# Moving the second routing exponential and two expert weight conversions on ScalarE

## Chip, cores and metric

The kernel runs on one core of a Trainium2 chip. The metric is the device time of one launch in microseconds (us). Engines are named as in the profile: PE is TensorE's matrix multiplication and PEld its weight load, DVE is VectorE, ACT is ScalarE, POOL is GpSimd, SP is SyncE, which here only issues transfers.

## What is computed

One decoder layer on 1,024 tokens (16 sequences of 64) of width 256: self-attention with 16 heads, then cross-attention, then a mixture of experts. The change lies in the last part, which in the reference is, cut to what matters:

```python
scores = softmax(xt @ Wg.T)                          # T x 16
gmask  = the 2 best of 4 groups of 4 experts
topi   = top 4 of the scores inside these groups
combine[t, topi] = scores[t, topi]
h = silu(xt @ W1[e].T) * (xt @ W3[e].T)              # 176 wide, each expert e
y = sum over e of combine[:, e] * (h @ W2[e].T)
z = silu(xt @ Ws1.T) * (xt @ Ws3.T) @ Ws2.T          # two shared experts, 352 wide
x = x + y + z
```

## The kernel before

**Precision.** Most products are made from two fp32r parts of each operand: a high part, written by ACT as a rounding copy, and a low part, written by DVE (or POOL) as source minus high part. A product is then three matmuls: high x high, high x low, low x high. `parts_of` (line 111) makes the two parts of an activation: the cast is line 112, the subtraction line 113. `weight_parts` (line 276) loads one expert's weights in one transfer of 640 KB on SP's queue (line 277), casts all 1,280 columns on ACT (line 278) and subtracts in two pieces (line 283): the first 768 columns on DVE, the last 512 on DVE for the first three experts and on POOL for all later ones.

**Order of the work.** The kernel is written as one program; a planner with a time model of its own sorts it, and each engine then runs its instructions strictly in the order so fixed. `tc.issue_after(ins)` adds an edge: what is traced in the block stays behind `ins` on the engine of `ins`, and nothing is said of other engines. The helper `after` takes several such instructions. So an edge permits or forbids places; it doesn't fix one.

**Routing.** Tokens are handled in two halves of 512. `choose` (from line 774) ranks the experts from the raw logits, so the softmax isn't needed for the choice. `send` scatters the token rows to per-expert slots in memory by indirect transfers that POOL issues (line 864), four for each of the four choices and half. `weights_of_choices` (line 891) makes the softmax: a maximum over the logits (line 897), a subtraction (line 899), the Exp on ACT (line 900), a sum, a reciprocal and a dozen small DVE operations (lines 902 to 919). Its results are used when the experts' outputs are added at the end, and by the dense expert's adds of that half.

**Around the change.** After cross-attention the two shared experts of the second half run: `shared_up` (Silu at line 937, a copy at 941), `shared_hidden` (product at 948, `parts_of`), `shared_output` (adds at line 970). The last of the 16 experts is dense (computed for all tokens): `dense_up`, `dense_gated`, `dense_out` (adds at line 974). Then 15 experts follow in a software pipeline over `e`, each on 384 slots:

- `expert_inputs` (from line 1309): a load `xr` of 408 KB on SP's queue (line 1314), which waits for the scatters of its choices; six PE transposes (line 1324); two casts (112), two subtractions (113).
- `expert_weights`, i.e. `weight_parts`; the raw weights have two buffers, so a load waits until the subtractions of two experts earlier are done.
- `expert_hidden` (from line 1333): 18 matmuls (through line 104), a Silu of the gate (line 1342), a DVE product (1343), `parts_of`, the same for the remaining 48 rows (Silu 1345, product 1346).
- `send_outputs` (from line 1352): 15 matmuls (line 104), three copies (line 1358), three indirect transfers that POOL issues (line 1363).

Before the change the weights of expert 1 and of expert 2 (the second and third; counting starts at 0) are cast after the latest second Silu (line 1345), because of `tc.issue_after(silus[-1])`; the second half's `weights_of_choices(1)` is traced as a whole in step `e == 1`, behind expert 0's gate.

Of the kernel before, what the change touches and what calls it, by code (L numbers as in the profile page):

```python
# [30 lines left out]
ALU = mybir.AluOpType  # L31
# [11 lines left out]
E, INTER, NGRP, TOPK, TOPKG = 16, 176, 4, 4, 2  # L43
# [28 lines left out]
def decoder_layer(ctx: ExitStack, tc: tile.TileContext, a: dict, out: bass.AP):  # L72
# [21 lines left out]
    @contextmanager  # L94
    def after(*instructions):

        with ExitStack() as order:
            for ins in instructions:
                order.enter_context(tc.issue_after(ins))
            yield  # L100
# [8 lines left out]
        return [(left[0], right[0]), (left[0], right[1]), (left[1], right[0])]  # L109

    def parts_of(src, hi, lo, eng=None):
        nc.scalar.copy(hi, src)
        return (eng or nc.vector).tensor_tensor(lo, src, hi, ALU.subtract).ins


    x_pairs = [acts.tile([128, 2, D], F32, tag=f"x{n}", name=f"x{n}") for n in range(NI // 2)]
# [198 lines left out]
    with ExitStack() as attn:  # L315
# [572 lines left out]
            nc.vector.tensor_tensor(w, w, p, ALU.mult)  # L888
            return w

        def weights_of_choices(half):


            shape = [128, 4, E]
            lg = logits[half]
            m = fs.tile([128, 4], F32, tag="r_m", name="r_m")
            nc.vector.tensor_reduce(m, lg, AX.X, ALU.max)
            p = fs.tile(shape, F32, tag=f"r_p{half}", name=f"r_p{half}")
            nc.vector.tensor_tensor(p, lg, m.unsqueeze(2).broadcast_to(shape), ALU.subtract)
            exps.append(nc.scalar.activation(p, p, AF.Exp).ins)  # L900
            s = fs.tile([128, 4], F32, tag="r_s", name="r_s")
            nc.vector.tensor_reduce(s, p, AX.X, ALU.add)
            nc.vector.reciprocal(s, s)
            nc.vector.tensor_tensor(p, p, s.unsqueeze(2).broadcast_to(shape), ALU.mult)
            sel = selected[half]
            last = fs.tile([128, 4], F32, tag=f"cl{half}", name=f"cl{half}")
            nc.vector.tensor_tensor(last, sel[:, :, E - 1], p[:, :, E - 1], ALU.mult)
            nth = fs.tile(shape, F32, tag="slot", name="nth_back")
            nc.vector.tensor_tensor(
                nth, places[half], sel[:, :, E - 1 :].broadcast_to(shape), ALU.add  # L910
            )
            ch = choices(nth, sel)
            kept = fs.tile(shape, F32, tag="slot", name="kept")
            nc.vector.scalar_tensor_tensor(kept, over[half], 0.5, p, ALU.is_lt, ALU.mult)
            nc.vector.tensor_tensor(
                ch, ch, kept.unsqueeze(1).broadcast_to([128, TOPK, 4, E]), ALU.mult
            )
            w = fs.tile([128, TOPK, 4], F32, tag=f"cw{half}", name=f"cw{half}")
            nc.vector.tensor_reduce(w, ch, AX.X, ALU.add)
            return w, last, p  # L920
# [23 lines left out]
        def shared_hidden(k, g, up, pool, h_p=None):  # L944

            n = min(128, SHI - k * 128)
            h = pool.tile([128, 512], F32, tag=f"rt{k % 2}0", name="sgh")[:n]
            nc.vector.tensor_tensor(h, up, g, ALU.mult)
            h_p = [
                t[:n]  # L950
                for t in h_p
                or [
                    pool.tile([128, 512], F32R, tag=f"c_t{m}", name=f"sh{m}", bufs=4)
                    for m in range(2)
                ]
            ]
            lows.append(parts_of(h, h_p[0], h_p[1]))
            return h_p

        def shared_output(half, hs):  # L960
            for k in range(4):
                ps = mm_tile(cols=D)
                cols = slice(k * 128, (k + 1) * 128)
                pairs = []
                for t, h_p in enumerate(hs):
                    n = min(128, SHI - t * 128)
                    pairs += three([p[:, cols] for p in h_p], [w[:n, t, :] for w in ws2_p])
                matmuls(ps, pairs)
                i = half * 4 + k
                nc.vector.tensor_tensor(x[i], ps, x[i], ALU.add)  # L970
# [10 lines left out]
        with (  # L981
# [150 lines left out]
            def dense_gated(g, up, g2, up2):  # L1132
                h_p = [
                    xa.tile([128, 512], F32R, tag=f"roped1{n}", name=f"dense1{n}", bufs=1)
                    for n in range(2)
                ]
                h_p.append(xa.tile([128, 512], F32R, tag="q_r", name="dense2"))
                nc.vector.tensor_tensor(g, up, g, ALU.mult)
                parts_of(g, h_p[0], h_p[1])
                nc.vector.tensor_tensor(g2[:64], up2[64:], g2[64:], ALU.mult)  # L1140
                parts_of(g2[:64], h_p[2][:64], h_p[2][64:])
                return h_p
# [18 lines left out]
            for n in range(len(units) + 2):  # L1161
# [85 lines left out]
                if n == 8:  # L1247
                    w_last = dense_weights()
                    with after(exps[-1]):
                        routed.append(weights_of_choices(0))  # L1250
                if n == 9:
                    rows[1] = [
                        xw.tile([128, 3, 2, 2, DC], F32, tag="w_s", name="rows1")
                        .rearrange("p a b c d -> p (a b c d)")[:, : 2 * ROW]
                        .rearrange("p (a b) -> p a b", a=2)
                        for _ in range(2)
                    ]
                    normed[1] = layernorm_t(3, (1,), token_rows(1))[0]
                    high = highs[-1]
                    scored, placed, aimed = choose(1)  # L1260
                    sh = [
                        xb.tile([128, 2, 2, 4 * HQ], F32R, tag=f"w_q{m}", name=f"sh{m}")
                        .rearrange("p a b c -> p (a b c)")
                        for m in range(2)
                    ]
                    hs = []
                    for k in range(3):
                        with after(*pn_turned[(0 if k else 1) :]):
                            up = shared_up(0, k, xa)
                            part = [t[:, k * 512 : (k + 1) * 512] for t in sh]  # L1270
                            hs.append(shared_hidden(k, *up, xa, part))
                    with tc.issue_after(rstds[-1]):
                        send(0, (2,), [lows[-1]])
                    with after(projected, scaled[-1]):
                        shared_output(0, hs)
                    send(0, (3,), [high])
                    send(1)
                    with after(high):
                        dense_ups = dense_up(0, turned[-1], scored, scored)
                    with after(aimed, scored):  # L1280
                        ups = [shared_up(1, 0, xa)]
                    with after(aimed, placed):
                        ups.append(shared_up(1, 1, xa))
                        hs = [shared_hidden(k, *ups[k], xa) for k in range(2)]
                        ups.append(shared_up(1, 2, xa))
                        hs.append(shared_hidden(2, *ups[2], xa))
                        h_p = dense_gated(*dense_ups)
                        shared_output(1, hs)
                        dense_out(h_p, 0, range(4), add_last)

# [121 lines left out]
    for e in range(E + 1):  # L1412
        if e in (1, 2):

            low = lows[-1]
            hs[e - 1] = expert_hidden(ws[e - 1], xs[e - 1][0], SLOTS)
        if e < E - 1:
            low = lows[-1]
            with tc.issue_after(up_done[0] if e in (1, 2) else low):
                xs[e] = expert_inputs(e)  # L1420
            if e >= 1:
                with tc.issue_after(low), tc.issue_after(silus[-1]):
                    ws[e] = expert_weights(a["W123"][e], nc.vector if e < 3 else nc.gpsimd)
        if e == 1:
            with tc.issue_after(gated[0]), tc.issue_after(silus[-1]):
                routed.append(weights_of_choices(1))
        if 0 <= e - 1 < E - 1 and e > 2:
            hs[e - 1] = expert_hidden(ws[e - 1], xs[e - 1][0], SLOTS)
        if e - 2 >= 0:
            if e == E:  # L1430

                with tc.issue_after(gated[0]):
                    h_p = dense_hidden(w_last, 1, 0)
            last = send_outputs(e - 2, ws.pop(e - 2), hs.pop(e - 2), xs.pop(e - 2)[1])
            if e - 2 == E - TOPK - 2:
                short = slots_are_short()
            k = e - 2 - (E - 1 - TOPK)
            if k >= 0:
                got[k] = load_outputs(k)
# [140 lines left out]
```

## Time and profile before

| | us |
|---|---|
| median of 3 runs (555.78 to 557.23) | 556.84 |
| the profiled execution's own time | 558.26 |
| its span, first to last instruction | 556.1 |
| busy of that span: PE / DVE / ACT / POOL | 524.9 / 382.5 / 304.3 / 228.7 |
| second half's shared experts, from their first matmul | 419.7 on |
| expert 0's first up matmul | 439.59 |
| experts 3 to 14 in a steady rhythm, about | 460 to 540 |

A line of a timeline gives the start in us from the span's start, the duration, engine, line, operation, what it writes <- what it reads (names without buffer numbers), the shape, how many were merged, and in brackets how long the engine was idle before and what ended that wait. "issue" there is a wait that the profile can't name. Times are of one profiled execution.

### The profile page before, as it was taken

To read this page: it belongs to the slowest core of one execution; us is meant where nothing else is said; L and a number is where in the kernel's file an instruction comes from. 1 tells how busy PE (TensorE), PEld (TensorE's weight loads), DVE (VectorE), ACT (ScalarE), POOL (GpSimd) and SP (SyncE) were. 2 spreads that over 40 slices of the span, in tenths; PEclk is the share of its full clock that TensorE was granted. 3 is DMA by queue.
4 is the path that set the end of the run, shared out by engine and by line. 5 is a ranking of instruction groups with operands and counts; after the bars stand their busy time and mean duration, and the time that the engine had idled before them with its cause. 6 is when DMAs were issued, how large, how long until landed. Compare 5 with 4: busy or idle time off the path is not lost.

```text
span 556.1 us, 10815 instructions
## 1 busy us (share of the span) xinstructions
PE 524.9 (94%) x4013; PEld 442.1 (80%) x4013; DVE 382.5 (69%) x863; ACT 304.3 (55%) x764; POOL 228.7 (41%) x213
## 2 busy tenths in 40 slices
PE   7999999999999989999999999999999879999982
PEld 6888898998989876668677686685886769999971
DVE  5465573754736799657475566758768688999967
ACT  3667575585665520625545364455735377777651
POOL 4260500101000016444342533543534737888873
PEclk9999999999999999999999999999999989999995
DMA  8553432834200779472010000000511577777366
GB/s 227 158 170 109 140 95 77 209 97 133 77 1 1 230 203 306 124 230 73 1 62 12 8 1 1 0 30 2 174 52 71 195 235 265 238 235 262 123 250 217
DMA packets 44263, 70.84 MB, mean 127 GB/s; under 512 B 11824, under 2 KB 25232, under 8 KB 44208
## 3 DMA queue, kind: packets, MB, share of 16 engines
q1 hardware_dynamic: 39376, 58.71, 35.3%
q0 software_dynamic: 3696, 10.36, 4.8%
q10 hardware_dynamic: 1136, 1.05, 0.6%
q8 instruction: 33, 0.54, 0.4%
q14 instruction: 22, 0.18, 0.1%
HBM read 48.61 MB, written 21.86 MB: 127 GB/s over the span
## 4 chain that ended last, share of the span: by engine, by line


## 5 line engine op out<-in xcount | busy, mean ns | idle before, releaser
L1014 POOL TENSOR_TENSOR roped<-rt,rt 128x512 f32<-128x512 f32 x48 | 61.8, 1309 | 52.6 <-DVE rt L1006 51.6
L104 PE MATMUL mm<-xn,w_q 128*128 128x512 f32 x288 | 72.6, 402 | 0.5 <-ACT xn L222 0.5
L1006 DVE TENSOR_TENSOR rt<-mm,rope_q 128x512 f32<-128x512 f32 x96 | 61.0, 680 | 10.8 <-PE mm L104 10.4
L104 PEld LDWEIGHTS mm<-xn,w_q 128*128 128x128 f32 x288 | 52.6, 188 | 14.3 <-issue 1.2
L104 PE MATMUL mm<-xs,w 128*128 128x384 f32 x270 | 53.8, 347 | 6.9 <-issue 2.3
L1363 POOL DMA_INDIRECT yd<-y,to x45 | 47.8, 1062 | 20.7 <-ACT y L1358 7.1
L325 DVE TENSOR_REDUCE sm_m<-at 128x8 f32<-128x512 f32 x32 | 21.9, 684 | 47.9 <-PE at L582 47.1
L104 PEld LDWEIGHTS mm<-xs,w 128*128 128x128 f32 x270 | 46.7, 192 | 9.0 <-issue 5.1
L331 ACT ACTIVATE p<-at,sm_m 128x64 f32<-128x64 f32 x128 | 38.2, 343 | 14.9 <-DVE sm_m L329 12.8
L523 POOL TENSOR_TENSOR wv<-code,scale 128x512 fp32r<-128x512 f32 x7 | 9.1, 1294 | 89.2 <-DMA scale<-in_scales 59.6
L1032 PE MATMUL mm<-roped,w_s 128*64 128x512 f32 x192 | 44.3, 599 | 0.2 <-DVE rt L1006 0.2
L360 ACT COPY pt<-at 64x512 f32<-64x512 f32 x32 | 18.6, 582 | 40.0 <-PE at L352 40.0
L565 ACT ACTIVATE qT<-mm,bqkv 128x512 f32<-128x512 f32 x32 | 21.8, 688 | 33.7 <-PE mm L104 33.7
L104 PE MATMUL mm<-wv,xn 128*128 128x256 f32 x256 | 36.2, 288 | 0.0
L104 PE MATMUL mm<-wo,o 128*128 128x256 f32 x256 | 34.1, 286 | 2.1 <-DVE x L624 2.1
L104 PE MATMUL av<-w,hp 128*128 128x256 f32 x225 | 35.1, 290 | 0.3 <-ACT y L1358 0.3
L104 PEld LDWEIGHTS mm<-wo,o 128*128 128x128 f32 x256 | 31.7, 191 | 3.7 <-DVE x L624 3.2
L104 PE MATMUL mm<-xn,wk 128*128 128x512 f32 x128 | 34.2, 399 | 0.0
L104 PE MATMUL mm<-xn,wq 128*128 128x512 f32 x128 | 33.2, 398 | 0.2
L343 POOL TENSOR_TENSOR pn<-p,sm_s 128x512 f32<-128x512 f32 x14 | 14.6, 1044 | 45.3 <-DVE sm_s L339 45.3
L104 PEld LDWEIGHTS mm<-wv,xn 128*128 128x128 f32 x256 | 32.5, 189 | 0.7
L601 PE MATMUL av<-pt,v 128*128 128x128 f32 x256 | 31.2, 275 | 1.0 <-DVE o L611 1.0
(219 smaller groups left out, 1184.3 us busy)
## 6 DMA issues: line engine op xcount, KB each, us to landing
w<-in_W SPq DMA_DIRECT2D x15, 640.0 KB
code<-in_codes SPq DMA_DIRECT2D x32, 256.0 KB
scale<-in_scales SPq DMA_DIRECT2D x32, 256.0 KB
xr<-xd SPq DMA_DIRECT2D x15, 408.0 KB
xd<-zeros SPq DMA_DIRECT2D x8, 720.0 KB
yd<-zeros SPq DMA_DIRECT2D x8, 512.0 KB
got<-yd SPq DMA_DIRECT2D x16, 256.0 KB
wq<-in_Wq SPq DMA_DIRECT2D x4, 512.0 KB
```

What stands on the lines that cost most here:

```text
L104: m = nc.tensor.matmul(ps, lhsT=l, rhs=r, start=(n == 0), stop=(n == len(pairs) - 1))
L325: nc.vector.tensor_reduce(m, sc, AX.X, ALU.max)
L331: last = nc.scalar.activation(p[:, b], sc[:, b], AF.Exp, bias=m[:, b : b + 1], accum_out=s[:, b : b + 1])
L343: .tensor_tensor(pn, p, s.unsqueeze(2).broadcast_to(shape), ALU.mult)
L360: nc.scalar.copy(pt[:S, :, 0, :], ps[:S])
L523: mults[n] = eng.tensor_tensor(w, *loaded[gr].pop(n), ALU.mult).ins
L565: nc.scalar.activation(qk[which][:, half * 512 : (half + 1) * 512], ps, AF.Identity, bias=bqkv[:, which, h : h + 1],).ins
L601: nc.tensor.matmul(av[:, k * 128 : (k + 1) * 128], lhsT=v[:, i, k0 : k0 + HD], rhs=pt[:, i].rearrange("p a q -> p (a q)"), start=True, sto ...
L1006: factors = nc.vector.tensor_tensor(mt, ps3, rope_table(t, 2 * ab + k), ALU.mult)
L1014: nc.gpsimd.tensor_tensor(r.rearrange("p (b s) -> p b s", s=S), one, two, op)
L1032: nc.tensor.matmul(ps[h // 2][(h % 2) * 64 : (h % 2) * 64 + 64], lhsT=w_s[:, t, blk, ab, :], rhs=roped[2 * t + ab], start=first[h], stop=l ...
L1363: sent = nc.gpsimd.indirect_dma_start(out=yd[: (E - 1) * SLOTS + min(TOPK, E - 1 - e) * NT], out_offset=bass.IndirectOffsetOnAxis(ap=to[:, ...
```

## The change

`weights_of_choices` is cut in two: `exps_of_choices` (maximum, subtraction, Exp) and the rest. For the first half both are called where the whole was. For the second half `exps_of_choices(1)` is called between the dense expert's gate and the shared experts' output, behind four instructions: the cast of the last shared hidden part, the dense gate's last cast and last subtraction, and the latest Silu. The casts of expert 1's and expert 2's weights get other edges: for expert 1 the cast must follow the last cast of expert 0's inputs instead of expert 0's second Silu; for expert 2 it must follow the last cast of expert 0's hidden part instead of expert 1's second Silu. Later experts keep their edges.

```diff
     def parts_of(src, hi, lo, eng=None):
-        nc.scalar.copy(hi, src)
-        return (eng or nc.vector).tensor_tensor(lo, src, hi, ALU.subtract).ins
+        high_last[0] = nc.scalar.copy(hi, src).ins
+        low_last[0] = (eng or nc.vector).tensor_tensor(lo, src, hi, ALU.subtract).ins
+        return low_last[0]
+
+    high_last, low_last = [None], [None]
...
-        def weights_of_choices(half):
-
+        def exps_of_choices(half):
 
             shape = [128, 4, E]
             lg = logits[half]
...
             exps.append(nc.scalar.activation(p, p, AF.Exp).ins)
+            return p
+
+        def weights_of_choices(half, p):
+
+
+            shape = [128, 4, E]
             s = fs.tile([128, 4], F32, tag="r_s", name="r_s")
...
-                        routed.append(weights_of_choices(0))
+                        routed.append(weights_of_choices(0, exps_of_choices(0)))
...
                         hs.append(shared_hidden(2, *ups[2], xa))
+                        order = [high_last[0]]
                         h_p = dense_gated(*dense_ups)
+
+                        with after(*order, high_last[0], low_last[0], silus[-1]):
+                            p_last = exps_of_choices(1)
                         shared_output(1, hs)
...
         if e in (1, 2):
 
-            low = lows[-1]
+            low, cast = lows[-1], high_last[0]
             hs[e - 1] = expert_hidden(ws[e - 1], xs[e - 1][0], SLOTS)
+            if e == 2:
+                cast = hidden_high
+            hidden_high = high_last[0]
         if e < E - 1:
...
             if e >= 1:
-                with tc.issue_after(low), tc.issue_after(silus[-1]):
+
+                with tc.issue_after(low), tc.issue_after(cast if e < 3 else silus[-1]):
                     ws[e] = expert_weights(a["W123"][e], nc.vector if e < 3 else nc.gpsimd)
         if e == 1:
             with tc.issue_after(gated[0]), tc.issue_after(silus[-1]):
-                routed.append(weights_of_choices(1))
+                routed.append(weights_of_choices(1, p_last))
```

## The prediction

> **What bounds the kernel now.** First the busy time in stretches of 10 us, to see where any engine has room. The columns are the stretch, its length, then busy us and instruction count of PE, PEld, DVE, ACT and POOL, the granted clock of PE, the DMA share and GB/s.
>
> ```profile
> 440.00:450.00 10.00, 8.08 (x48) 7.05 (x47) 6.86 (x21) 6.19 (x11) 6.81 (x7) 1.00 0.78 261
> 450.00:460.00 10.00, 7.60 (x41) 6.77 (x41) 7.51 (x18) 7.03 (x13) 2.96 (x3) 0.83 0.77 248
> 460.00:470.00 10.00, 10.00 (x71) 9.97 (x70) 8.40 (x16) 7.46 (x18) 7.63 (x7) 1.00 0.69 241
> 479.00:540.00 61.00, 59.23 (x407) 57.34 (x407) 54.16 (x94) 42.49 (x94) 50.79 (x43) 1.00 0.65 222
> ```
>
> From 460 on PE is nearly always busy, and in the 61 us from 479 POOL has 43 instructions with 10.2 us between them, 0.24 each, which is the gap (0.16 to 0.30) that it leaves between any two: POOL is full there as well. So the rhythm of the later experts has no slack, and what counts is when it starts. Between 440 and 460 PE idles 1.92 + 2.40 = 4.3 us, and for a part of that time its clock is low. That is the place of the change. Next, ACT's timeline there, of which the lines that carry the argument are:
>
> ```profile
> 447.41 0.51 ACT L112 CAST hp<-h 64x384 fp32r<-64x384 f32 x1
> 447.94 1.28 ACT L900 ACT_TABLE_LOAD   x1
> 449.31 0.26 ACT L900 ACTIVATE r_p<-r_p 128x64 f32<-128x64 f32 x1
> 449.59 1.28 ACT L1342 ACT_TABLE_LOAD   x1
> 450.88 0.49 ACT L1342 ACTIVATE g<-mm 128x384 f32<-128x384 f32 x1
> 451.40 0.48 ACT L1345 ACTIVATE g<-mm 64x384 f32<-64x384 f32 x1
> 451.90 1.26 ACT L278 CAST w<-w 128x1280 fp32r<-128x1280 f32 x1
> 453.07 0.47 ACT L112 CAST xs<-at 128x384 fp32r<-128x384 f32 x1
> ...
> 457.68 1.26 ACT L278 CAST w<-w 128x1280 fp32r<-128x1280 f32 x1 [2.40 <-DMA w<-in_W]
> ```
>
> ACT is never idle from 447.41 to 453.5, and expert 2's input cast (453.07) is last in that row. PE's timeline shows who waits for it, and SP's when expert 3's weights are asked for:
>
> ```profile
> 450.17 0.82 PE L1324 MATMUL at<-ident,xr 128*128 128x128 f32 x6
> 450.74 0.72 PE L104 MATMUL av<-w,hp 128*128 128x256 f32 x4
> 453.59 0.80 PE L104 MATMUL mm<-xs,w 128*128 128x384 f32 x3 [2.13 <-ACT xs L112]
> ...
> 446.64 4.39 SPq L1314 DMA_DIRECT2D xr<-xd  x2
> 451.54 0.33 SPq L277 DMA_DIRECT2D w<-in_W  x1
> ```
>
> Expert 2's tokens are transposed by 451.0 but cast only at 453.07. Expert 3's weights, asked for at 451.54, let ACT cast them only at 457.68.
>
> **The change, part by part.** *The Exp's removal from 447.94.* Two table loads and the Exp, 1.28 + 0.26 + 1.28 with their small gaps, hold ACT from 447.94 to 450.88, 2.94 us. Not all is a gain: expert 1's gate product, which the Silu at 450.88 needs, ends at about 449.65 by PE's timeline (the ninth of the matmuls from 447.18 and two of those from 449.12), so the Silu alone gains 1.2 us. The rest of the hole serves the next edit.
>
> *Expert 2's weight cast ahead of expert 1's Silus.* It may now follow the cast at 447.41. Its data were asked for at 440.22, and the DMA share shows that load done before 445. So it fits from 447.94 to 449.20, into the hole, costs nothing there, and leaves 451.90. Then Silus at 449.66 and 450.36, input cast at 450.84 instead of 453.07: 2.23 us. If the planner left the cast where it is, only the Exp's 1.2 us would remain. Its low part (two DVE instructions of 0.94 and 0.68, overlapping to 1.55 us) moves along; DVE has 2.5 us idle between 450 and 460 and 3.1 in the ten before.
>
> *Expert 1's weight cast ahead of expert 0's Silus.* Its data were loaded at 396.75. ACT is idle from 440.28 to 442.55 and takes the 1.26 us there. After the Silu at 443.19 the input casts are then free of it, and DVE's 1.55 us for its low part (444.98 to 446.54, right in front of the inputs' low part that PE waits for until 447.18) moves to 441.5 to 443.1, where DVE idles 2.13 us. PE waits 1.11 and 0.49 us in this stretch. Both could go, 1.6. But expert 1's second input cast starts at 447.04 after 1.24 us in which ACT waited for something that the profile calls "remote"; its transposes had ended at 444.3. If that wait stays, PE stops again before 447.5 and the gain is 0.3. Between 0.3 and 1.6 I take 0.6, nearer to the end at which the wait stays, for nothing in the change touches it.
>
> *The Exp's new place.* Behind the shared experts' last cast, which starts at 433.92 and takes 0.62, ACT idles until 439.06: 4.5 us, room for a load and the Exp (1.6). Its two small DVE operations (0.22 and 0.22) fall behind 431.09, where DVE idles 0.42, 0.22 and 1.50 us before 435.4; cover enough, and 0.4 us on the shared adds at 438.34 if it were gone. What is not free is the reload for Silu. At 449.59 the reload began as soon as the Exp was done; in the new order the instruction before expert 0's Silu is the weight cast, which ends at 441.54, and 1.28 more gives 442.82 against 442.55 now: 0.27 lost. The Trainium skill (ScalarE: Activation LUTs, "What ACT_TABLE_LOAD costs") speaks against the place: it counts a drain of about 1.38 us on top of each load, 2.66 a switch. By that rule the Silu would come at 444.2, 1.65 us late, and eat most of the first edits' gain. The rows here show no drain: a load ends at 449.22 and the Exp starts at 449.31, the next load ends at 450.87 and the Silu starts at 450.88. I take the rows, 0.27.
>
> *What PE gains at expert 2's first matmul:* 2.23 + 0.6 - 0.27 = 2.6 us. Expert 2's transposes then come at about 449.8 instead of 450.17, as their load, asked for at 446.64, allows.
>
> *The clock.* The windows of single microseconds behind 455 show it:
>
> ```profile
> 455.00:456.00 1.00, 1.00 (x8) 0.73 (x7) 0.97 (x3) 0.27 (x1) 0.84 (x1) 0.68 0.86 317
> 456.00:457.00 1.00, 1.00 (x5) 1.00 (x6) 0.97 (x4) 0.00 (x0) 0.85 (x1) 0.50 1.03 157
> 457.00:458.00 1.00, 1.00 (x5) 1.00 (x4) 0.88 (x2) 0.33 (x1) 0.17 (x1) 0.50 0.74 289
> 458.00:459.00 1.00, 1.00 (x5) 1.00 (x4) 0.04 (x1) 1.00 (x2) 0.00 (x0) 0.62 0.97 379
> ```
>
> PE was granted half speed for about 3.4 us, with work all the time: 1.7 us lost. The Trainium skill (TensorE: Matmul & The Clock Gate, Part 1) says that a free-running window of 3.4 us of low activity sets this; the stretch before it holds the wait of 2.13 us. By the rule the change would avoid the drop, by the rows alone it could equally fall elsewhere: 0 to 1.7. I take it as gone, since the wait goes; so PE could be ahead by up to 2.6 + 1.7 = 4.3 us before expert 3.
>
> *What is late next.* Expert 3's weights. SP's queue is in order, and their load stands behind expert 3's tokens, which wait at 450.72 for the last scatter (POOL ends it at 448.64); the change moves no scatter. If that order stays, the weights still land near 457.6, POOL's subtraction on them still starts at 459.02, and all sends behind it in POOL's queue start where they do now. Then only POOL's waits after that, beyond its own gaps, can shrink: at 466.28, 472.40 and 478.07 it waited 1.43, 0.91 and 0.82, less 0.30 each: 2.3 us. If the planner, whose view of expert 1's subtraction is now earlier, puts the load ahead of that token load, or a send ahead of that subtraction (0.96 + 0.30 = 1.26 each), more of the 4.3 is kept. I take 2.3 plus one such send, 3.5, less 0.3 for the low DVE slack (DVE would have to run above 90% from 443 on): **3.2 us**.
>
> Sum: span 556.1 - 3.2 = 552.9, the profiled execution's own time 558.26 - 3.2 = 555.1. That execution is 1.42 above the median of the runs, so the median becomes 556.84 - 3.2 = 553.6.
>
> **The rivals.** *All of it is kept.* Expert 3's weights come early; PE's 4.3 plus the rest of its 1.6 before expert 1 arrive at the end: about 5 us, 551.8. For it speaks that expert 1's raw buffer is free 3 us earlier; against it DVE, which has under 6% to spare later.
>
> *Given back at expert 3's weights.* The queue stays, and POOL's three waits shrink by half only, as each is ended by another engine: 1.2 us, 555.6. For it speaks the row at 457.68. Near it lies the case that the casts are not moved and the Exp's 1.2 us are all.
>
> *POOL's queue falls out of step; slower.* New edges change the planner's times, and so the order of ACT's and POOL's instructions far behind the edits. POOL is full from 479 to 540 with nine subtractions on expert weights (L283) in its queue, each behind a cast on ACT. If a cast comes late in each expert, POOL waits, and the sends and the next load wait behind it. At 459.02 such a wait took 1.85 us. With 0.6 us for each of nine experts it is 5.4 us: 553.6 + 5.4 = 559.0. It decides from 3.2 / 9 = 0.36 us an expert on. Against it: ACT is only 70% busy there, and those later edges are the old ones.
>
> **How the numbers follow.** 0.3% is 1.67 us, about what a measurement of this kernel can tell from no change: below 555.2 is faster, above 558.5 slower. Likeliest 0.39 (553.6, its own range 552.0 to 555.0), all kept 0.18, given back 0.25 (a third of it below 555.2), out of step 0.18 (a sixth of it under 558.5). Faster: 0.38 + 0.18 + 0.08 = 0.64; slower 0.15; the rest 0.21. The range reaches from 551.2, with the upper half of the DVE doubt in the second case, to 558.0, over the third case and the mild part of the fourth; about 0.07 is left below and 0.13 above.
>
> **What would show it.** In the changed profile: table load and Exp at about 434.5 in ACT's idle time; weight casts at about 440.3 and 448 in front of Silus; no wait near 2 us of PE for expert 2's input cast; no stretch of low clock at 455 to 459; expert 3's cast either still waiting for its DMA near 457.6 (given back) or not; POOL's full stretch beginning some 3 us earlier with waits of 0.16 to 0.30. I would be wrong if the scatters, and not ACT, set expert 2's start, if the reload costs more than the rows show, or if POOL waits for casts in the steady rhythm.

## The result and the profile after

The changed kernel takes 558.92 us (median of 17 runs, 555.21 to 561.88), the kernel before, on the same chip, 556.03 (17 runs). The ratio is 1.0052 with a 95% interval of 1.0035 to 1.0068: 2.9 us slower, where 3.2 us faster was predicted. The profiled execution took 558.92, its span is 556.7.

The windows of 10 us that answer to those of before (stretch, length, then busy us and count of PE, PEld, DVE, ACT and POOL, the granted clock of PE, DMA share, GB/s):

```profile
440.00:450.00 10.00, 7.09 (x44) 6.36 (x44) 9.75 (x28) 7.45 (x15) 6.58 (x7) 1.00 0.60 209
450.00:460.00 10.00, 7.55 (x35) 7.47 (x36) 5.24 (x8) 2.49 (x7) 2.34 (x2) 0.66 0.84 300
460.00:470.00 10.00, 10.00 (x72) 9.96 (x71) 8.91 (x17) 7.41 (x17) 6.26 (x6) 1.00 0.54 188
475.00:536.00 61.00, 58.79 (x410) 57.27 (x409) 54.48 (x92) 43.65 (x94) 50.20 (x42) 1.00 0.64 220
```

PE still idles between 440 and 460, now 2.9 + 2.5 = 5.4 us, and its clock in the second of these windows is lower than it was, 0.66. ACT and POOL, the engines that the change was to relieve, are at a quarter of that window. ACT's timeline shows that the edits themselves did what they say:

```profile
430.52 1.28 ACT L902 ACT_TABLE_LOAD   x1
431.82 0.26 ACT L902 ACTIVATE r_p<-r_p 128x64 f32<-128x64 f32 x1
...
434.39 1.27 ACT L281 CAST w<-w 128x1280 fp32r<-128x1280 f32 x1
437.98 1.28 ACT L1354 ACT_TABLE_LOAD   x1 [2.32 <-PE mm L104]
439.27 0.49 ACT L1354 ACTIVATE g<-mm 128x384 f32<-128x384 f32 x1
...
441.87 1.27 ACT L281 CAST w<-w 128x1280 fp32r<-128x1280 f32 x1
...
445.97 0.86 ACT L112 CAST xs<-at 128x384 fp32r<-128x384 f32 x2 [0.52 <-PE at L1336]
...
448.07 1.27 ACT L281 CAST w<-w 128x1280 fp32r<-128x1280 f32 x1
```

The Exp runs behind the shared experts; expert 1's and expert 2's weights are cast at 434.39 and 441.87, ahead of Silus; expert 2's inputs are cast as soon as PE has transposed them. One line at the end is new: 448.07 is the cast of expert 3's weights, which before waited for its data until 457.68. PE, over the next stretch:

```profile
446.52 0.78 PE L104 MATMUL mm<-xs,w 128*128 128x384 f32 x3
447.16 1.18 PE L104 MATMUL av<-w,hp 128*128 128x256 f32 x7
452.45 0.88 PE L1336 MATMUL at<-ident,xr 128*128 128x128 f32 x3 [4.11 <-DMA xr<-xd]
```

Expert 2's up product has begun (three matmuls at 446.52), all its operands are there, and PE stands still for 4.11 us: the next instruction in its queue is the first half of expert 3's transposes, whose tokens have not come. Expert 2's other 15 up matmuls are queued behind it. SP's timeline says when those tokens were asked for, and the chain of work that ended last what they waited for:

```profile
441.88 0.32 SPq L1326 DMA_DIRECT2D xr<-xd  x1
442.33 0.34 SPq L280 DMA_DIRECT2D w<-in_W  x1
448.76 0.83 SPq L1326 DMA_DIRECT2D xr<-xd  x2
449.71 0.36 SPq L280 DMA_DIRECT2D w<-in_W  x1
```

The chain's pieces at that place (start, us, what):

```profile
443.87 4.33 DMA xd<-rows,to
448.76 3.55 DMA xr<-xd
```

The weight load of expert 3 is at 442.33, ahead of its token load at 448.76; before, it stood behind. It now runs beside the last scatters. The last scatter, issued at 443.87, takes 4.33 us to land, and the tokens take 3.55 more. POOL then pays for PE's standstill:

```profile
460.09 0.96 POOL L1375 DMA_INDIRECT yd<-y,to  x1 [7.58 <-ACT y L1370]
```

To compare executions, I cut the time at the first up matmul of an expert on PE. Expert 0 began at 434.35 against 439.59, but 4.0 of these 5.2 us lie ahead of the first scatter of the second half (422.77 against 426.80), where nothing was changed; in the undisturbed executions below, of either order, that scatter starts anywhere from 422.8 to 427.2. The other 1.2 us are no gain of the change either: behind that scatter expert 0 starts after 11.6 us in the changed kernel, after 11.6 in e6, which has PE's order of before up to expert 2, and after 12.8 in the profiled execution of before. So only what follows expert 0's start is compared. Kernels e1 to e16 are told below.

| us | to expert 2 | 2 to 3 | 3 to 4 | 4 to 14 | 14 to end | sum |
|---|---|---|---|---|---|---|
| before | 14.00 | 7.07 | 7.02 | 58.34 | 30.12 | 116.55 |
| changed | 12.17 | 11.97 | 7.03 | 59.22 | 31.96 | 122.36 |
| changed, again (e13) | 12.62 | 9.95 | 7.05 | 59.23 | 32.03 | 120.88 |
| e1, Exp alone | 16.33 | 5.60 | 6.81 | 58.11 | 31.49 | 118.35 |
| e2, casts alone | 13.76 | 10.02 | 6.69 | 58.61 | 32.26 | 121.35 |
| e15, order of before | 14.54 | 7.18 | 7.04 | 58.03 | 32.19 | 118.98 |
| e14, changed, tokens freed | 12.61 | 5.07 | 7.32 | 59.32 | 31.93 | 116.25 |
| e3, weight load behind | 12.31 | 9.14 | 7.16 | 58.94 | 32.36 | 119.92 |
| e8, PE kept busy | 11.98 | 9.91 | 6.24 | 58.54 | 31.76 | 118.43 |
| e4, up product first | 12.38 | 7.48 | 5.71 | 58.39 | 32.08 | 116.05 |
| e16, as e4 | 12.60 | 7.44 | 5.71 | 59.17 | 31.50 | 116.42 |
| e5, both orders | 12.55 | 7.76 | 7.79 | 58.37 | 32.00 | 118.47 |
| e6, before, up product first | 14.65 | 6.65 | 5.92 | 60.78 | 31.97 | 119.97 |

The change gains 1.8 us up to expert 2 and loses 4.9 from expert 2 to expert 3. It loses another 0.9 in the rhythm of the later experts. Each row is one execution: between e13 and e15, on one chip, the same three figures are 1.9, 2.8 and 1.2. The last column before the sum is no part of it: the tail of the profiled execution of before was short (30.12), that of e15, in the same order, is 32.19.

### The profile page after: what moved, and what is told of

The parts are those of the page before. It is cut to its first block, busy times and chain, and to the rows that moved or that the text cites. A ratio compares the mean times of both kernels' runs of the same rounds, so it can differ in the third digit from the quotient of the medians.

```text
span 556.7 us, 10813 instructions
## 1 busy us (share of the span) xinstructions
PE 524.6 (94%) x4013; PEld 443.2 (80%) x4013; DVE 386.0 (69%) x863; ACT 304.6 (55%) x764; POOL 228.9 (41%) x213
## 4 chain that ended last, share of the span: by engine, by line
PE 75%; DVE 9%; DMA 5%; POOL 4%; issue 4%; ACT 3%; SPq 0%; DVEq 0%; ACTq 0%; POOLq 0%
PE mm L104 43%; PE mm L1040 8%; PE av L604 5%; PE at L585 3%; PE av L104 3%; PE at L355 3%; PE av L1078 3%; POOL xd L867 3%; PE at L1065 2%; DVE rt L1014 2%; PE mm L465 1%; PE mm L443 1%; DMA xd<-rows,to 1%; ACT w L281 1%; POOL yd L1375 1%
## 5 line engine op out<-in xcount | busy, mean ns | idle before, releaser
L104 PE MATMUL mm<-xs,w 128*128 128x384 f32 x270 | 55.6, 352 | 4.5 <-ACT w L281 2.4
L1375 POOL DMA_INDIRECT yd<-y,to x45 | 47.8, 1062 | 24.5 <-ACT y L1370 11.6
L113 DVE TENSOR_TENSOR hp<-h,hp 128x384 fp32r<-128x384 f32 (+3 forms) x34 | 30.8, 907 | 2.9 <-ACT hp L112 2.0
```

Source lines behind the costliest of these rows:

```text
L104: m = nc.tensor.matmul(ps, lhsT=l, rhs=r, start=(n == 0), stop=(n == len(pairs) - 1))
L113: low_last[0] = (eng or nc.vector).tensor_tensor(lo, src, hi, ALU.subtract).ins
L1375: sent = nc.gpsimd.indirect_dma_start(out=yd[: (E - 1) * SLOTS + min(TOPK, E - 1 - e) * NT], out_offset=bass.IndirectOffsetOnAxis(ap=to[:, ...
```

## The experiments

**Theory.** The gain arrives at expert 2 and is lost to expert 3's tokens: they depend on the last four scatters, which the change moves no earlier; the weight load that now runs beside those scatters makes them later still; and PE's queue has expert 3's transposes in front of work that is ready. The long standstill then halves PE's clock for 6.8 us. **Rivals.** The order of the later experts, which the planner changed too, costs the time (POOL or PE waiting for casts in each expert). Or expert 3's weights are what is late, as the prediction had it.

### One part at a time

e1_exp_only moves only the Exp; e2_casts_only moves only the casts:

```diff
 # e1_exp_only
-                with tc.issue_after(low), tc.issue_after(cast if e < 3 else silus[-1]):
+                with tc.issue_after(low), tc.issue_after(silus[-1]):
 # e2_casts_only
-                        with after(*order, high_last[0], low_last[0], silus[-1]):
-                            p_last = exps_of_choices(1)
...
-                routed.append(weights_of_choices(1, p_last))
+                routed.append(weights_of_choices(1, exps_of_choices(1)))
```

> Only the Exp of the second half is moved; the two weight casts keep the edges of before, so SP's order of loads and nearly all of the later order of PE, DVE and ACT are those of before. Theory A (the loss sits at expert 3: its tokens wait for the last scatter, and PE's queue has their transposes in front of most of expert 2's up product): expert 2 starts up to 1.2 us earlier, and as expert 3's tokens come when they came before, part of it is lost in front of them: 0 to 1 us faster than before, 555 to 556. Theory B (the loss comes from the changed order of the later experts): this order is not changed, so the full 1.2 us, about 554.8. If it is slower than before by 2 us or more, the Exp's new place is the cause and both are wrong.

Measured: 556.57, ratio 0.9998 (0.9976 to 1.0021). The time is near what theory A gave, but not for its reason. Expert 2 starts 2.3 us later than before (16.33 against 14.00), where up to 1.2 us sooner was expected: the Silu of expert 0 now has its table load in front, expert 1's weight cast still stands ahead of its input casts, PE waits 2.03 us for them at 442.51, and its clock is half from 444.3 to 447.8. From expert 2 to 3, where the half clock of before lay, 1.5 us come back.

> Only the two weight casts are moved; the Exp stays in expert 1's stage. SP then has expert 3's weights ahead of expert 3's tokens, as in the changed kernel, and the later order changes too. Theory A: as slow as the changed kernel or up to 1.5 us better, since PE comes to expert 3's transposes later and waits less there: 557 to 559. Theory B: about as slow as the changed kernel, 558 to 560.

Measured: 559.30, ratio 1.0047 (1.0032 to 1.0061). That is above the 557 to 559 of theory A and inside the range of B, so this run doesn't decide between them. The loss comes with the casts. With them the planner puts expert 3's weight load ahead of its tokens, as in the changed kernel (expert 2 to 3 takes 10.02 us); with the Exp alone it does not (5.60). At expert 2 the two parts don't add up: the casts alone gain 0.2 us, the Exp alone loses 2.3, both together gain 1.8.

### The order on SP and on PE

e3_load_behind changes one place in SP's queue: expert 3's weight load goes behind its token load. e4_up_first changes PE's queue instead: expert 3's inputs are transposed behind the whole of expert 2's up product. In its edit `silu` keeps expert 3's weight cast behind the same Silu as before. e5_both does both.

```diff
 # e3_load_behind
+        inputs_load[0] = load
...
+                    with after(*([inputs_load[0]] if e == 3 else [])):
                         ws[e] = expert_weights(...)
 # e4_up_first
-        if e in (1, 2):
+        silu = silus[-1]
+        if e in (1, 2, 3):
...
-            with tc.issue_after(up_done[0] if e in (1, 2) else low):
+            with tc.issue_after(up_done[0] if e in (1, 2, 3) else low):
...
-                with tc.issue_after(low), tc.issue_after(cast if e < 3 else silus[-1]):
+                with tc.issue_after(low), tc.issue_after(cast if e < 3 else silu if e == 3 else silus[-1]):
```

> The changed kernel, in which SP's queue has expert 3's weights behind expert 3's tokens again, as before the change; no other instruction changes its place. Theory A with contention (the 640 KB that are asked for at 442.3 delay the last scatters and so the tokens): tokens land 1 to 2 us earlier relative to the first scatter, PE's wait of 4.1 us shrinks to 2 to 3, and the time falls by 1 to 2.5 us against the changed kernel, to about 557. Theory A without contention: no earlier tokens, and the weights come late on top: no gain, 559 to 560. Theory B: no change.

Measured: 558.07, ratio 1.0024 (1.0002 to 1.0045). PE's timeline of this kernel has at expert 3's transposes:

```profile
452.50 0.65 PE L1338 MATMUL at<-ident,xr 128*128 128x128 f32 x3 [1.92 <-DMA xr<-xd]
```

And ACT:

```profile
456.23 1.27 ACT L281 CAST w<-w 128x1280 fp32r<-128x1280 f32 x1 [5.81 <-DMA w<-in_W]
```

By ratio that is 0.28% under the changed kernel, but the two intervals overlap, so a gain is not shown. PE's standstill falls from 4.11 to 1.92 us: the tokens are asked for 1.6 us after the last scatter's instruction ends, against 3.5 in the changed kernel and 2.1 before. The other pair that differs in this load alone has the same figures, 3.5 in e4 and 1.6 in e5. So the weight load did delay the scatters beside it. The Trainium skill (DMA: Bandwidth & Descriptors, SWDGE vs HWDGE vs iDMA) has the transfers of GpSimd and of SyncE in different queues of the same engines, served in turn, which fits. But now the weights are late, and ACT, which is to cast them next, stands still for 5.81 us. The order on SP only chooses which of the two is late.

> The changed kernel, with expert 3's transposes behind expert 2's whole up product in PE's queue (they stood in front of 15 of its 18 matmuls). Theory A: PE does 2.6 us of that product while the tokens come, its wait falls from 4.1 to about 1.5 us, the half clock of 6.8 us shrinks or goes, and the time falls to 552 to 554.5, where the prediction had it. Theory B: the order of later experts is almost that of the changed kernel, so 558 to 559.5.

Measured: 554.71, ratio 0.9952 (0.9932 to 0.9972), faster than both kernels and 0.2 us above the expected range. PE's timeline:

```profile
456.09 0.85 PE L1336 MATMUL at<-ident,xr 128*128 128x128 f32 x6 [1.42 <-DMA xr<-xd]
```

PE's line at expert 3's transposes shows that the tokens are as late as in the changed kernel, but PE works on expert 2 meanwhile, waits 1.42 us, and its clock stays whole until the tail.

> The changed kernel with two orders changed: PE multiplies expert 2's whole up product ahead of expert 3's transposes, and expert 3's weight load goes out behind its token load on SP. The first alone gave 554.71 and left PE a wait of 1.42 us for expert 3's tokens at 456.1. If the early weight load is what makes those tokens late (1.9 us between the changed kernel and the one with the load behind), the wait of 1.42 goes, and about 1 us more is gained: 553.2 to 554.3. If instead the weights of expert 3 then become late (the predicted limit), PE or POOL waits for their cast and it gives nothing or costs a little: 554.7 to 556.5.

Measured: 557.67, ratio 1.0013 (0.9997 to 1.0030). Both ranges were missed: it is slower than either. Against e4 only the place of that one load was edited, and this line of ACT answers:

```profile
453.14 1.26 ACT L281 CAST w<-w 128x1280 fp32r<-128x1280 f32 x1 [3.39 <-DMA w<-in_W]
```

Expert 2's Silus, whose products PE had finished, stood behind this cast, and PE then waited 1.75 us for expert 3's input cast and had 3.4 us of half clock. So the early weight load is needed as well: it is the half of the change's side effects that helps, once PE has work while the tokens come.

### Is it PE's order by itself?

e6_before_up_first makes the edit of e4 in the kernel before, e7_exp_up_first in e1.

> The kernel before with the same change of PE's order alone: expert 2's whole up product ahead of expert 3's transposes. In the kernel before PE reached those transposes at 455.92 and hardly waited for their tokens. If the order of PE is what the change brought to light, it gives nothing here: 555.8 to 557.3. If the order of PE gains by itself (by the stretch of half clock, or by later order), it gives about what it gave on top of the change: 553.5 to 555.

Measured: 559.06, ratio 1.0045 (1.0028 to 1.0061).

> Only the Exp is moved, both weight casts stay where they were, and PE multiplies expert 2's whole up product ahead of expert 3's transposes. It tells what the two weight casts are worth once PE's order lets their gain through. By my local account (3.0 us at expert 2's first matmul with all, 1.2 from the Exp's place alone) the casts are worth about 1.8, less what the late tokens take: 555.5 to 556.5 here against 554.71 with the casts. If the casts are worth nothing or less than nothing, this is 554.7 or below.

Measured: 559.36, ratio 1.0051 (1.0029 to 1.0072). Neither expectation for e6 was right, nor either of those for e7: both are slower. So e7 doesn't tell what the casts are worth. By the table, expert 4 starts 0.9 us sooner in e6 than before (27.22 against 28.09), but experts 4 to 14 then take 60.78 us, 2.4 more; e7 has the same 60.78. These are the windows of that stretch (columns as above), before, in the changed kernel and in e6:

```profile
467.70:526.00 58.30, 56.86 (x388) 55.39 (x386) 54.60 (x95) 43.61 (x92) 48.58 (x40) 1.00 0.66 221
465.50:524.70 59.20, 56.86 (x388) 55.35 (x386) 55.18 (x93) 43.20 (x90) 48.51 (x40) 1.00 0.64 217
461.90:522.70 60.80, 57.82 (x392) 55.75 (x390) 55.85 (x96) 44.24 (x92) 47.24 (x40) 1.00 0.65 217
```

PE stands idle for 1.4 us of it before, 2.3 in the changed kernel and 3.0 in e6. In e6 this line names most of it (what waited, for whom: us in total, times, longest):

```profile
PE mm L104 <- ACT w L278: 2.1, 4, 0.6
```

Here the rival's mechanism is seen at work. An edit in the middle moves the planner's order of the casts far behind it, and PE waits for late casts: that is 1.5 of the 2.4 us of e6; the other 1.0 is more PE work in this stretch, whose cause is open. So e4's gain is not PE's order by itself: the same edit on the old casts costs 2.5 us. In the changed kernel the whole 0.9 us is idle time of PE, of which the same line names 1.8 us of 2.3; whether all of it is the order's stays open, for the same program gave 58.39 in e4 and 59.17 in e16.

### The clock

e8_filler gives PE 28 transposes of the identity, whose result is overwritten, just ahead of expert 3's transposes:

```diff
+            for n in range(28 if e == 3 and c == 0 else 0):
+                nc.tensor.transpose(ps[:, n % 3 * 128 : n % 3 * 128 + 128], ident, ident)
```

> The changed kernel with 28 transposes of the identity on PE just ahead of expert 3's transposes, in the tile that those then overwrite: work whose result is never used, in the time in which PE waited 4.11 us for expert 3's tokens. They fill some 3 us. If the half clock behind that wait is a part of the loss (6.8 us at half speed against none, up to 3.4 us), the clock stays whole from 451 on and the time falls to 556 to 557.3. If only the wait itself costs, it stays at 558.5 to 560.

Measured: 557.01, ratio 1.0008 (0.9992 to 1.0023).

```profile
448.50 3.22 PE L1336 MATMUL at<-ident 128*128 128x128 f32 x28
452.49 0.87 PE L1338 MATMUL at<-ident,xr 128*128 128x128 f32 x6 [0.78 <-DMA xr<-xd]
453.12 2.85 PE L104 MATMUL mm<-xs,w 128*128 128x384 f32 x15
```

The real work starts no sooner than in the changed kernel (452.49 against 452.45), but the 15 matmuls behind take 2.85 us, where the changed kernel has 3.23 for nine and 2.05 for six, 2.4 more. In e13, the changed kernel again, they take 3.19 and 1.29, 1.6 more than here. So some 2 us of the loss are the half clock; a part may be later order, which moved too. The runs of the changed kernel point the same way: the eight with a mean granted clock of 0.984 or more took 555.21 to 558.04 us, the nine with 0.982 or less 558.92 to 561.88. But in the 22 runs of e13 time and clock hardly go together, so this size stays rough. These are single microseconds of the changed kernel, with the clock in the last but two columns:

```profile
452.00:453.00 1.00, 0.55 (x4) 0.58 (x4) 0.97 (x2) 0.00 (x0) 0.51 (x1) 0.50 1.15 411
...
457.00:458.00 1.00, 1.00 (x5) 1.00 (x4) 0.61 (x2) 0.84 (x2) 0.00 (x0) 0.50 0.53 220
458.00:459.00 1.00, 1.00 (x8) 1.00 (x7) 0.58 (x2) 0.43 (x2) 0.00 (x0) 0.93 0.00 0
```

### Freeing the tokens

In e10_after_tokens and e11_before_tokens expert 3 computes on expert 2's token rows, so that its load needn't wait for the last scatters (its own rows are left out of the result); e9_both_cast_behind is e5 with expert 3's weight cast behind expert 2's Silus; e12_up_first_again is e4.

```diff
+        rank = 2 if e == 3 else e
-        first = TOPK * NT + (E - 2 - e) * SLOTS
+        first = TOPK * NT + (E - 2 - rank) * SLOTS
...
-        for k in range(min(TOPK, e + 1)):
+        for k in range(min(TOPK, rank + 1)):
             behind(load, sent_for[k])
...
```

> As e5_both (expert 2's whole up product ahead of expert 3's transposes, expert 3's weight load behind its tokens), but ScalarE casts expert 3's weights behind expert 2's two Silus instead of ahead of them. In e5_both ScalarE waited 3.39 us for those weights with the Silus, expert 3's input cast and what PE needs of them behind it. If that wait at the head of ScalarE's queue is what made e5_both slower (557.67) than e4_up_first (554.71), which differs from it in nothing but that one load's place, this takes back most of the 3 us: 554 to 555.8. If the late weights hold up expert 3 in whatever order they are cast, it stays at 556.5 to 558.5. Orders further behind change too, which can blur it by 2 us, as in e6_before_up_first.

> The changed kernel, but expert 3 computes on expert 2's token rows (its own rows are left out; its send targets are loaded apart, 384 numbers, behind expert 4's tokens), so that neither its tokens nor what follows them on SP waits for the last four scatters. If expert 3's late tokens and the half clock behind them are what cost the change its gain, PE's wait of 4.11 us goes and the time falls to 553 to 555.8. If not they but the new order of the later experts cost it, it stays at 558 to 560.

> The kernel before with the same (expert 3 on expert 2's rows). There PE waited for ScalarE and not for expert 3's tokens, though ScalarE waited 2.40 us for expert 3's weights, whose load stands behind those tokens; so it should gain little: 554.8 to 556.8. With e10_after_tokens it makes the pair without the late tokens: if I am right, the change is worth 1 to 3 us there, in the way that the prediction had it; if the change is worth nothing there either (the two within 0.3%), what it did locally doesn't reach the end for another reason.

> e4_up_first once more, beside the others on one chip, since e5_both and e4_up_first were on two chips: 0.993 to 0.998 of the kernel before if the gain holds (553.5 to 555.7); above 556 if the first result was a lucky chip.

Measured: ratios 1.0008 (0.9988 to 1.0029), 1.0037 (1.0011 to 1.0062), 0.9996 (0.9979 to 1.0012) and 0.9987 (0.9963 to 1.0011), against 563.95 us of the kernel before. e12 misses its range, and e10 against e11 has the sign of the rival. But these runs don't settle it. On that chip ACT, and in three of the kernels DVE too, stood still just ahead of expert 0, ACT for 6.88 us in e11, 9.49 in e10, and longest in e12 (13.79):

```profile
448.84 0.86 ACT L112 CAST xs<-at 128x384 fp32r<-128x384 f32 x2 [13.79 <-remote]
```

The scatters went on meanwhile, so expert 3's tokens were no longer late in relation to PE. The loss of e10 against e11 lies ahead of expert 0, which starts 19.3 us behind the first scatter against 15.1; from there to expert 14, e10 takes 3.2 us less. Why this standstill was longer in the changed order is not known, and on such a chip the change is no gain even with the tokens freed. What e9 was to tell of e5 stays open.

Three of them were therefore run on another chip, beside the changed kernel:

> The changed kernel, as the control of the three beside it: 1.0035 to 1.007 of the kernel before.

> The changed kernel with expert 3 computed on expert 2's token rows (its own are left out), as e10_after_tokens. If the late tokens cost the change its gain: PE's wait of 4.11 us and the second half of the half clock go, and about 3 us come back, 0.994 to 0.9995 of the kernel before. If the order of the later experts costs it: 1.003 to 1.007.

> The kernel before with the same: it hardly waited for expert 3's tokens, so 0.9965 to 1.0005 of the kernel before. If late tokens are the cause, e14_after_tokens is below this by 1 to 3 us; if not, above it or level.

> The changed kernel with expert 2's whole up product ahead of expert 3's transposes, as e4_up_first: 0.993 to 0.998 of the kernel before if its gain holds, 0.998 to 1.001 if it is that of e12_up_first_again.

| | us | ratio to before | interval |
|---|---|---|---|
| e13, changed | 561.30 | 1.0043 | 1.0021 to 1.0065 |
| e14, changed, tokens freed | 557.24 | 0.9963 | 0.9943 to 0.9983 |
| e15, before, tokens freed | 559.23 | 0.9998 | 0.9980 to 1.0017 |
| e16, changed, up product first | 556.71 | 0.9930 | 0.9903 to 0.9957 |

PE at expert 3's transposes in e13:

```profile
451.46 1.18 PE L104 MATMUL av<-w,hp 128*128 128x256 f32 x7
455.76 0.58 PE L1336 MATMUL at<-ident,xr 128*128 128x128 f32 x3 [3.12 <-DMA xr<-xd]
```

And in e14:

```profile
450.96 1.19 PE L104 MATMUL av<-w,hp 128*128 128x256 f32 x7
451.99 0.49 PE L1338 MATMUL at<-ident,xr 128*128 128x128 f32 x3
452.24 1.81 PE L104 MATMUL mm<-xs,w 128*128 128x384 f32 x9
```

All four ratios lie in the ranges given for the theory. Freeing the tokens takes 4.1 us (561.30 - 557.24) from the changed kernel and nothing measurable from the one before. Without the late tokens the change is a gain, 559.23 - 557.24 = 2.0 us, though the later experts of e14 keep the order's 59.32 us. This decides between the theory and the rival of the later order: the tokens turn the sign. One reservation: in e14 the planner also put expert 3's weight load behind its tokens again; in e3 that alone went with 0.28%, not clear of noise, and can be a share of the 4.1 us. The clock goes with the tokens. The windows of e15 and of e14 at this place:

```profile
454.00:458.00 4.00, 3.90 (x18) 3.64 (x17) 3.90 (x7) 1.96 (x3) 3.10 (x3) 0.57 0.85 229
449.00:457.00 8.00, 7.99 (x55) 7.54 (x56) 7.24 (x17) 6.50 (x16) 4.46 (x4) 1.00 0.80 267
```

e15 has 3.4 us of half clock there, as before; e14 has none up to its tail. And e16 confirms e4: with PE's queue reordered the change runs in 0.993 of the kernel before.

## Why the prediction was wrong, step by step

**The Exp's removal and expert 2's cast: right.** They went where the prediction put them, and from expert 1's first up matmul to expert 2's PE took 5.70 us instead of 8.16. That is 2.46, and 1.9 between e13 and e15 (6.25 against 8.18), where 2.23 was predicted. The two parts hold only together: with the Exp alone (e1) this stretch took 8.70.

**The reload for Silu: the term 0.27 was too small.** I let the load begin as soon as the instruction before it was done, as at 449.59 before. The line 437.98 shows otherwise: ACT waited 2.32 us for PE's product, and only then loaded. The rows of before could not show this: at 449.59 the product was due within 0.1 us (449.65 in the prediction's reading). ACT in e13, which has the load there:

```profile
441.70 1.28 ACT L1354 ACT_TABLE_LOAD   x1 [1.83 <-PE mm L104]
```

And in e15, which hasn't:

```profile
441.53 0.49 ACT L1358 ACTIVATE g<-mm 128x384 f32<-128x384 f32 x1 [3.19 <-PE mm L104]
```

e13's Silu then starts at 443.00, 4.82 us behind expert 0's first matmul; e15's 3.52. The price is 1.30, the load in full. The Trainium skill (ScalarE: Activation LUTs, "What ACT_TABLE_LOAD costs") would make it 2.66; its drain of 1.38 is not in these rows (the load ends at 439.26, the Silu starts at 439.27). The gain at expert 2 is 1.8 to 1.9 us (before and changed, e15 and e13), 0.7 to 0.8 under the 2.6; from e6, whose order is that of before up to there, to e5 and e8 on its chip it is 2.1 to 2.7 (14.65 against 12.55 and 11.98).

**Expert 1's cast: 0.6 was predicted, and it is eaten by the reload.** The "remote" wait that I let stand is gone (the second input cast, at 441.08, follows its neighbour at once), but PE still waits 1.38 us at 440.82, for input casts behind the late Silu. From expert 0 to expert 1 PE took 6.47 us against 5.84 before, but the order of before took 6.47 in e6 and 6.36 in e15, and e13 took 6.37. So by the first pair the cast gives back 0.7 of the 1.3 us that the reload costs, by the others all of it.

**The clock: 1.7 us were to be gained, and nothing was.** The wait of 2.13 us went, but a standstill replaced it. With its 4.11 us the half clock lasts 6.8 us (451.3 to 458.1), which loses as much again; with the 3.12 us of e13 it lasts 3.4, as before. Where the standstill is gone (e14) or short (e4 and e16), the clock stays whole, as the prediction wanted. The rule of the Trainium skill (TensorE: Matmul & The Clock Gate, Part 1), windows of about 3.4 us, agrees with these lengths. The longest waits beside them: 1.75 to 3.12 us with 3.4 us of half clock in seven traces (before, e1, e3, e5, e7, e13, e15), 2.10 us with 6.8 in e2, but 1.92 us with none in e6; none with waits of up to 1.42 us (e4, e8, e14, e16).

**"What is late next": this step failed.** I named expert 3's weights, and wrote that if the planner put their load ahead of the token load, more of the gain would be kept. It did put it there, and the sign was the opposite. I had the tokens in the same sentence, waiting for the last scatter, and saw in them only what holds up the weights in SP's queue. But PE's timeline of before has expert 3's transposes, at 455.92, ahead of 15 of expert 2's 18 up matmuls, of which three ran at 453.59:

```profile
455.92 0.90 PE L1324 MATMUL at<-ident,xr 128*128 128x128 f32 x3
456.47 2.86 PE L104 MATMUL mm<-xs,w 128*128 128x384 f32 x9
```

With PE earlier they become its next limit: the tokens, bound to the last scatter, could not follow, and the term put at nothing, PE's wait for them, measured 4.11 us (3.12 in e13). In the new order the load also delayed them, by 1.4 us against before. The weights did matter, as e3 and e5 show, but as the second of two late transfers.

**The rivals.** Late casts in the rhythm exist, and alone make e6 slower; in the changed kernel they are at most 0.9 us (1.2 between e13 and e15), with PE and not POOL waiting. In time the result fell where that rival was placed (559.0), by chance: the larger part of the loss has another reason.

## What to carry over

When work is moved earlier, go through each in-order queue behind it and ask of every instruction, not only of the next operand, when its data can come: PE's next instruction may belong to another expert. A wait at the head of PE's queue can cost more than its length: behind most of the waits from 1.75 us on PE's clock was half for 3.4 us or more. Putting ready work ahead was worth 4.6 us (e13 against e16), where mending the transfer's order only moved the wait to ACT. After any such edit compare the order on the transfer queue and of the later casts first: a planner may move what the diff doesn't name.

## What was not expected of the hardware

In its new place the table load for Silu ran only when the wait for PE's product was over, in every trace that has it (1.28 us behind waits of 1.83 to 3.47), so the wait did not hide it. That is no rule for table loads: e15 has one ahead of the wait of its activation,

```profile
445.52 1.28 ACT L900 ACT_TABLE_LOAD   x1
448.26 0.26 ACT L900 ACTIVATE r_p<-r_p 128x64 f32<-128x64 f32 x1 [1.45 <-DVE r_p L899]
```

and so has e6. What decides it is not known. One weight load of 640 KB beside the last scatters made the next read of their rows start 1.9 us later in the two pairs that differ in its place alone (3.5 against 1.6 us behind the last scatter's instruction). And one chip had ACT idle for 6.88 to 13.79 us at one place in all four kernels traced there, put down to "remote"; its cause was not found.
